# Splitting a turned block in two steps placed apart, and loading copied inputs ahead of copied states, in a recurrence and binary-FFN kernel

## The chip, the cores and the metric

The kernel runs on one core of one Trainium2 chip. The metric is the device time of one execution in microseconds (us). Three runs of the kernel before gave 456.02, 456.13 and 455.75 us; their median is 456.02 us.

## What is computed

`x` has shape (2, 4096, 256). A gated recurrence of state width 64 runs along the 4096 steps, its output is projected and normalised, and a feed-forward network with weights reduced to sign times mean magnitude follows.

```python
u = x @ W_in + b_in
g = sigmoid(x @ W_gate + b_gate)
h_t = tanh(h_prev @ A + u_t @ Bm)
y_t = h_t @ C.T + u_t @ D.T
y_t = g_t * y_t + (1.0 - g_t) * x_t
x1 = layernorm(x + (y @ W_out + b_out + x))
bw = mean(abs(w), axis=1) * sign(w)          # for w1 and for w2
h = gelu(x1 @ bw1.T + b1)                    # exact gelu, width 1024
out = layernorm(x1 + (h @ bw2.T + b2))
```

## The kernel before, in words

**Tiling.** The 4096 steps are cut into 64 segments of 64 steps that run side by side, so one recurrence step handles 2 x 64 columns at once. The plan is 48 warm-up steps and then 64 real ones. The 8192 rows of the output are worked on in 16 chunks of 512 rows (`NC` = 16, `SPC` = 4 recurrence steps to a chunk).

**Recurrence.** `steps` (L156) is one matmul of `ab` with the tile `st` (L157), which holds the states h in its upper 64 partitions and the inputs u in its lower 64, and one tanh on ACT that writes the next h (L158). The matmul of a step needs the tanh of the step before it.

**A chunk's stations.** `load` (L343) copies four steps of h and u out of `st` into `hu` by two DMAs. `mix` (L369) multiplies `hu` with `cd` into the PSUM tile `ps_y` (L374) and subtracts x into `d` on DVE (L381). `mix_end` makes y in the tile `tg` (L386, L389). `project` (L392) multiplies y with `w_out` into `ps_z` (L399), adds it into `xn` on DVE (L410) and takes the statistics of the first layernorm (`all_stats` L283: bn_stats L256, aggregate L260, variance plus eps L265, and a power of -1/2 on POOL L266). `shift` is a small DVE operation `nm_a` (L271), and `norm` applies scale and shift on ACT (L279). The normed block must then be turned. For chunks 2 to 14 `blocks` (L441) does this by a transpose within 32 x 32 blocks on DVE (`xb`, L446) and 16 DMAs of 32 KB from the SP queue (L452) that put the blocks in place in `xlo`. For the other chunks `turn` (L422) uses TensorE. `split` (L458) makes the high part `xhi`, a rounded copy on ACT (L460), and the low part, `xlo` minus `xhi`, on DVE (L461), in place.

**Feed-forward.** `up(g)` for g = 0 to 3 (L470) makes two tiles of hidden units: for each, products of the sign weights with `xhi` and then with `xlo` into `ps_h` (L479) and a gelu on ACT (L489), and after the second a rounded copy `hhi` on ACT (L500). `low(g)` (L503) makes `hlo` on DVE (L507). `down(g)` (L565) multiplies `hhi` and `hlo` into `ps_o` (L523), and after the last group `scale` writes `o` on DVE (L539). `add` (L543) adds it to the row, `stats` takes the second layernorm's statistics (`bs_b`, `rs_b`, `nm_b`), and `store` (L554) applies them on ACT (L279) and issues the output DMA (L560) on the SP queue. `rest` (L465) is an addition of a bias row on POOL.

**The order.** Every engine has one queue that it works off in order. Under `manual_schedule` (L689) the order on each is the order in which this Python code emits instructions. The loop over `c` (L759 to L818) works in iteration c on the FFN of chunk c, finishes the FFN of chunk c-1, mixes and projects chunk c+2, and normalises, turns and splits chunk c+1, which is "far" when 0 < c < 14 (L760). Four recurrence steps are emitted in an iteration by `step()` (L768, L779, L807, L812), named A, B, C and D here, until the plan is used up. In iteration c the matmul order is: up 0, step A, down 2 of c-1, mix of c+2, up 1, step B, down 3 of c-1, one gate tile (c from 1 to 12), up 2, step C, down 0, project of c+2, up 3, step D, down 1. `split` for chunk c+1 is called from within up 3, between its two gelus, through the argument `between` (L496, L811).

**Buffers named below.** `ps_h` rotates through 3 buffers that it shares with the gate tiles, `ps_y` and `ps_z` of the loop share one, `ps_o` has one, `h` has two, `xhi` and `xlo` two each, `hu` three.

**Before the loop**, gate tiles of later chunks are emitted in small pieces by `parts(n, pace)` between recurrence steps, and chunks 0, 1 and 2 are loaded by `next_steps` as soon as their states are there (L649 to L651).

## Time and profile before

| what | value |
|---|---|
| median of three runs | 456.02 us (455.75 to 456.13) |
| the profiled execution's own time | 453.23 us |
| its span, from first to last instruction | 451.5 us |
| TensorE matmul busy | 430.5 us, 95% of the span |
| VectorE (DVE) busy | 332.3 us, 74% |
| ScalarE (ACT) busy | 284.2 us, 63% |
| GpSimd (POOL) busy | 158.9 us, 35% |
| mean granted TensorE clock | 0.995 |
| share of DMA queue q1 in 16 engines' span | 35.4% |

The profiled execution lies 2.79 us below the median of the runs, so differences are worked out against 453.23 us and then carried over to the median. 1.73 us of the profiled time lie outside its span. A line of the profile's group view names the source line, the engine, the operation, the tile written and the tiles read, then busy time and the mean length of one in ns, then the idle time of the engine just before it and what ended that. PE is TensorE's matmul, PEld its weight load, SPq the SyncE queue that issues DMAs. In timelines the first number is the start in us from the span's start and the second the length. Matmul ends are modelled, so PE counts as busy also where it is not at its peak.

From one iteration to the next the kernel before takes 23.13 us (DVE's L461 starts at 127.75 us in iteration 1 and at 266.52 us in iteration 7).

### The profile page before, as it was taken

How to read it: one execution, taken by the hardware profiler on the slowest of the kernel's cores; microseconds unless marked ns; L12 is line 12 of the kernel's file. 1: busy time of each engine (PE TensorE's matmuls, PEld its weight loads, DVE VectorE, ACT ScalarE, POOL GpSimd, SP SyncE). 2: the span in 40 equal slices, each digit the busy share in tenths (PEclk: the TensorE clock that was granted, in tenths of full speed). 3: DMA queues.
4: the chain of work that ended last, by engine and by line, in shares of the span. 5: the costliest groups of instructions: out<-in, count | busy, mean ns of one | idle time of the engine just before them, and what ended most of it. 6: DMA issues, size and time to landing. Idle time of an engine off the chain costs nothing.

```text
span 451.5 us, 6834 instructions
## 1 busy us (share of the span) xinstructions
PE 430.5 (95%) x2402; PEld 344.3 (76%) x2402; DVE 332.3 (74%) x571; ACT 284.2 (63%) x476; POOL 158.9 (35%) x177
## 2 busy tenths in 40 slices
PE   9999998999999999999999999999999999988992
PEld 5665766788878787888878787878787878777982
DVE  0245937966979797878787888888787878785874
ACT  2443541577585859595858676767676767757681
POOL 1000500644352526161615261525252525241613
PEclk9999999999999999999999999999999999999998
DMA  8887514500253424252426241615142323210102
GB/s 300 301 276 256 216 23 131 173 1 6 54 161 70 185 65 143 59 195 53 158 46 213 45 166 42 215 42 169 40 131 77 95 69 87 74 64 1 46 1 99
DMA packets 31480, 51.34 MB, mean 114 GB/s; under 512 B 5329, under 2 KB 19665, under 8 KB 31441
## 3 DMA queue, kind: packets, MB, share of 16 engines
q1 hardware_dynamic: 30864, 50.48, 35.4%
q8 instruction: 21, 0.34, 0.4%
q10 hardware_dynamic: 576, 0.37, 0.3%
q14 instruction: 19, 0.15, 0.1%
HBM read 31.43 MB, written 8.39 MB: 88 GB/s over the span
## 4 chain that ended last, share of the span: by engine, by line
PE 40%; DVE 38%; issue 6%; POOL 5%; ACT 3%; SPq 3%; DMA 2%; DVEq 0%; POOLq 0%; ACTq 0%
PE ps_o L523 8%; PE ps_h L479 8%; PE ps_g L313 7%; PE ps_y L374 6%; POOL rs_b L266 5%; DVE bs_b L256 4%; PE ps_s L157 4%; DVE xlo L461 4%; DVE d L386 4%; PE ps_u L131 3%; DVE bs_a L256 3%; DVE o L539 3%; DVE d L381 3%; DVE xn L545 3%; DVE tg L389 3%
## 5 line engine op out<-in xcount | busy, mean ns | idle before, releaser
L489 ACT ACTIVATE h<-ps_h,bias_c,al 128x512 f32<-128x512 f32 x128 | 97.4, 776 | 39.6 <-PE ps_h L479 34.2
L523 PE MATMUL ps_o<-sg,hhi 128*128 128x256 f32 x496 | 121.5, 286 | 0.5 <-DVE o L539 0.5
L523 PE MATMUL ps_o<-sg,hlo 128*128 128x256 f32 x496 | 118.1, 279 | 0.1
L523 PEld LDWEIGHTS ps_o<-sg,hhi 128*128 128x128 f32 x496 | 93.5, 189 | 1.7 <-DVE o L539 0.9
L523 PEld LDWEIGHTS ps_o<-sg,hlo 128*128 128x128 f32 x496 | 93.5, 188 | 1.2 <-DVE hlo L507 0.4
L479 PE MATMUL ps_h<-xhi,sg 128*128 128x512 f32 x256 | 93.0, 445 | 0.5 <-ACT xhi L460 0.5
L479 PE MATMUL ps_h<-xlo,sg 128*128 128x512 f32 x256 | 81.5, 399 | 8.4 <-DVE xlo L461 8.2
L507 DVE TENSOR_TENSOR hlo<-h,hhi 128x1024 fp32r<-128x1024 f32 (+1 forms) x65 | 79.0, 1219 | 5.4 <-ACT hhi L500 5.3
L359 POOL TENSOR_TENSOR xn<-xn,bo_r 128x256 f32<-128x256 f32 x64 | 47.5, 774 | 84.8 <-DMA xn<-in_x 75.6
L266 POOL TENSOR_TENSOR rs_b<-rs_b,neg_half 128x4 f32<-128x4 f32 (+1 forms) x17 | 27.3, 1606 | 134.6 <-DVE rs_b L265 134.3
L500 ACT CAST hhi<-h 128x1024 fp32r<-128x1024 f32 (+1 forms) x65 | 67.5, 1040 | 2.0
L313 PE MATMUL ps_g<-xt,w_gate 128*128 128x384 f32 (+3 forms) x208 | 66.4, 431 | 0.0
L479 PEld LDWEIGHTS ps_h<-xlo,sg 128*128 128x128 f32 x256 | 47.1, 188 | 24.4 <-DVE xlo L461 13.8
L359 POOL TENSOR_TENSOR xn<-xn,b_r 128x256 f32<-128x256 f32 x64 | 61.6, 993 | 2.0 <-PE ps_t L427 2.0
L479 PEld LDWEIGHTS ps_h<-xhi,sg 128*128 128x128 f32 x256 | 46.5, 189 | 19.1 <-issue 11.2
L158 ACT ACTIVATE st<-ps_s 64x128 f32<-64x128 f32 x112 | 30.1, 268 | 47.6 <-PE ps_s L157 47.3
L399 PE MATMUL ps_z<-w_out,tg 128*128 128x256 f32 x256 | 58.2, 379 | 0.0
L157 PEld LDWEIGHTS ps_s<-st,wab 128*128 128x128 f32 x224 | 38.5, 189 | 22.4 <-ACT st L158 9.7
L279 ACT ACTIVATE xn<-xn,nm_b,rs_b 128x256 f32<-128x256 f32 x58 | 30.3, 594 | 40.1 <-DVE nm_b L271 40.1
L399 PEld LDWEIGHTS ps_z<-w_out,tg 128*128 128x128 f32 x256 | 47.2, 190 | 5.7
L157 PE MATMUL ps_s<-st,wab 128*128 128x128 f32 x224 | 43.9, 278 | 0.1
L381 DVE TENSOR_TENSOR d<-ps_y,xt 128x1024 f32<-128x1024 f32 x16 | 19.6, 1225 | 28.2 <-PE ps_y L374 28.2
(76 smaller groups left out, 465.3 us busy)
## 6 DMA issues: line engine op xcount, KB each, us to landing
xt<-in_xT SPq DMA_DIRECT2D x35, 512.0 KB, 4.3
xn<-in_x SPq DMA_DIRECT2D x16, 512.0 KB, 3.3
out_y<-xn SPq DMA_DIRECT2D x15, 512.0 KB, 2.6
xlo<-xb SPq DMA_DIRECT2D x208, 32.0 KB, 1.9
hu<-st SPq DMA_DIRECT2D x32, 128.0 KB, 2.3
w1t<-in_w1T SPq DMA_DIRECT2D x2, 512.0 KB, 5.8
w1n<-in_w SPq DMA_DIRECT2D x2, 512.0 KB, 7.4
w2t<-in_w2T SPq DMA_DIRECT2D x2, 512.0 KB, 6.0
```

The source lines that it names most:

```text
L157: nc.tensor.matmul(p_h, ab, st[:, j].rearrange("p b k -> p (b k)"), start=True, stop=True)
L256: nc.vector.bn_stats(self.bs[:, i, :], self.r[:, i, :])
L266: nc.gpsimd.tensor_tensor(rs, rs, neg_half[:, cut], ALU.pow)
L313: nc.tensor.matmul(ps[:, cut], w_gate[:, k, bass.ts(m, P)], xt_[:, k, cut], start=k == 0 and i == 0, stop=k == KD - 1, skip_group_check=True,)
L359: nc.gpsimd.tensor_tensor(r[:, i, :], r[:, i, :], row, ALU.add)
L381: nc.vector.tensor_sub(self.d, ps, xt_)
L399: nc.tensor.matmul(self.ps_z[:, i, :], self.y[:, k, bass.ts(i, P)], w_out[:, k, :], start=k == 0, stop=k == KD - 1,)
L479: nc.tensor.matmul(ps, sg1[:, k, bass.ts(j, P)], part[:, k, :], start=n == 0, stop=n == 2 * KD - 1,)
L489: nc.scalar.activation(to, ps.rearrange("p (a i c) -> p a i c", a=P // 32, c=32) if self.far else ps, AF.Gelu, bias=b1_c[:, j : j + 1], sc ...
L500: nc.scalar.copy(hi[:, part, :], h[:, part, :])
L507: nc.vector.tensor_sub(lo[:, i, :], h[:, i, :], hi[:, i, :].bitcast(FP))
L523: nc.tensor.matmul(ps[:, i, :], part[:, j % 2, bass.ts(tb, P)], sg2[:, j, :], start=j == 0 and part is self.h[j // 2][0] and first, stop=j ...
```

## The change

- `split` becomes `split_hi` (the ACT copy) and `split_lo` (the DVE subtraction). `split_hi` is emitted right after up 2, so on ACT it stands behind the copy `hhi` of up 2 and ahead of the store of chunk c-1; before, it stood between the two gelus of up 3.
- The statistics of the first layernorm leave `project` and become `stats1`. `split_lo` is emitted between the two, so on DVE the order is `xn` (L410), `xlo`, `bs_a`, where it was `xn`, `bs_a`, `mv_a`, `rs_a`, `xlo`.
- `low` of group 2 goes ahead of the store's shift `nm_b` on DVE.
- `load` becomes `load_u` and `load_h`. The u half is issued first; for chunks 0 to 2 it is issued with the `load_n` calls ahead of the last warm-up steps, and only the h half waits for the states.
- Ahead of the loop one piece of gate work moves: two pieces instead of one after the mix of chunk 0, and one instead of two after the projection of chunk 1.
- In iteration 13 `low` of group 0 goes ahead of the mix of chunk 15, and the four small DVE operations of `compare` move from iteration 13 to iteration 14.

The diff, cut to its core:

```diff
-        def load(self):
-            c, nm = self.c, self.nm
-            self.hu = xp.tile([P, N], FP, tag="hu", name=f"hu{nm}", bufs=3)
-            for r, src in (
-                (TOP, h_of[:, bass.ds(c * SPC + 1, SPC)]),
-                (LOW, u_of[:, bass.ds(c * SPC, SPC)]),
-            ):
-                nc.sync.dma_start(out=self.hu[r, :], in_=src.rearrange("p j b k -> p (j b k)"))
+        def load_u(self):
+            self.hu = xp.tile([P, N], FP, tag="hu", name=f"hu{self.nm}", bufs=3)
+            src = u_of[:, bass.ds(self.c * SPC, SPC)]
+            nc.sync.dma_start(out=self.hu[LOW, :], in_=src.rearrange("p j b k -> p (j b k)"))
+
+        def load_h(self):
+            src = h_of[:, bass.ds(self.c * SPC + 1, SPC)]
+            nc.sync.dma_start(out=self.hu[TOP, :], in_=src.rearrange("p j b k -> p (j b k)"))
 
         def load_n(self):
             c, nm = self.c, self.nm
...
             if half == 1:
                 x1 = self.x1 = self.xn
                 nc.vector.scalar_tensor_tensor(x1, self.xn, 2.0, self.ps_z, ALU.mult, ALU.add)
-                self.st1 = all_stats(x1, f"a{nm}")
+            yield
+
+        def stats1(self):
+            self.st1 = all_stats(self.x1, f"a{self.nm}")
             yield
 
         def shift(self):
...
                     )
             yield
 
-        def split(self):
+        def split_hi(self):
             self.hi = wk.tile([P, KD, N], FR, tag="xhi", name=f"xhi{self.nm}")
             nc.scalar.copy(self.hi, self.lo.bitcast(FP))
+            yield
+
+        def split_lo(self):
             nc.vector.tensor_sub(self.lo, self.lo.bitcast(FP), self.hi.bitcast(FP))
             self.h = {}
             self.far = True
+            yield
 
         def rest(self):
 
             self.add_row(self.x1, b2_r)
             yield
 
-        def up(self, g, apart=False, between=None):
+        def up(self, g, apart=False):
             nm = f"{self.nm}_{g}"
             h = wk.tile([P, 2, N], FP, tag="h", name=f"h{nm}")
             hi = wk.tile([P, 2, N], FR, tag="hhi", name=f"hhi{nm}", bufs=3)
...
                     bias=b1_c[:, j : j + 1],
                     scale=al1[:, j : j + 1],
                 )
-                if i == 0 and between is not None:
-                    between()
                 if i == 1:
                     for part in range(2) if apart else [slice(0, 2)]:
                         nc.scalar.copy(hi[:, part, :], h[:, part, :])
...
             first_states()
         for i in range(3):
             if done == WARM + (i + 1) * SPC:
-                ch[i].load()
+                ch[i].load_h()
         for what, args in waiting or ():
             what(*args)
         if waiting:
...
             need = WARM + (ch[i].c + 1) * SPC
             while done < need:
                 next_steps()
-            ch[i].load()
+            ch[i].load_u()
+            ch[i].load_h()
         elif what in ("load_n", "load_x", "load_gate_x"):
             getattr(ch[i], what)()
         else:
...
                 load_xT(n + 3)
                 for i in ((0,), (1, 2))[n - 5]:
                     ch[i].load_n()
+                    ch[i].load_u()
             for i in range(7 - before):
                 if 1 <= n < 5 and i == 0:
                     load_w(n - 1)
...
             ch[i].xt = x_tiles[i]
         do(0, "mix", pace=850)
         do(0, "mix_end")
-        parts(1, 600)
+        parts(2, 600)
         assert done >= WARM + 2 * SPC, done
         do(1, "mix", pace=850)
         do(1, "mix_end")
         parts(1, 600)
         do(0, "project", 0, p_2, "o", pace=1700)
         do(0, "project", 1, pace=1700)
+        do(0, "stats1")
         assert done >= WARM + 3 * SPC, done
         do(2, "mix", pace=1700)
         do(0, "shift")
         do(1, "project", 0, p_2, "o", pace=1700)
         do(0, "norm")
         do(1, "project", 1, pace=1700)
+        do(1, "stats1")
         mixed = ch[2].mix_end()
         next(mixed)
-        parts(2, 1700)
+        parts(1, 1700)
         while waiting:
             next_steps()
         waiting = None
...
             do(c, "up", 0)
             step()
             do(c - 1, "down", 2)
+            if c == end - 2:
+                do(c, "low", 0)
             if c > 0:
                 do(c + 2, "mix")
                 do(c + 2, "mix_end")
-            do(c, "low", 0)
+            if c != end - 2:
+                do(c, "low", 0)
+            if c == end - 1:
+                next(parts_met)
+                next(parts_met)
             do(c + 3, "load")
             do(c + 6, "load_x")
             if c % 2 == 0:
...
             if not far:
                 do(c + 1, "turn")
             do(c, "low", 1)
+            if c == end - 1:
+                next(parts_met)
+                next(parts_met)
             if not 1 <= c <= 12:
                 add()
             do(c + 1, "rest")
             do(c, "up", 2)
+            if far:
+                do(c + 1, "split_hi")
+            do(c, "low", 2)
             if c < end - 1:
                 do(c - 1, "store", range(TB), nc.scalar)
                 do(c + 3, "load_n")
-            do(c, "low", 2)
             if c == end - 1:
                 do(c - 1, "stats")
             if c == end - 2:
                 assert done == len(plan), done
-                next(parts_met)
-                next(parts_met)
             step()
             do(c, "down", 0)
             do(c + 2, "project", 0)
             do(c + 2, "project", 1)
-            do(c, "up", 3, False, ch[c + 1].split if far else None)
+            if far:
+                do(c + 1, "split_lo")
+            do(c + 2, "stats1")
+            do(c, "up", 3)
             step()
             do(c, "down", 1)
             if c == end - 1:
                 do(c - 1, "store")
-            if c == end - 2:
-                next(parts_met)
-                next(parts_met)
         count()
         do(end, "up", 0)
         do(end - 1, "low", 3)
```

More of the change, by code (lines that the diff above doesn't have):

```diff
@@ L619, in redo @@
             self.load_x()
-            self.load()
+            self.load_u()
+            self.load_h()
             self.load_n()
             pieces = [self.gate, self.mix, self.mix_end, lambda: self.project(0), lambda: self.project(1)]
+            pieces += [self.stats1]
             pieces += [self.shift, self.norm, self.turn, self.rest]
```

## Prediction

> **What bounds the kernel now.** I read the list of waits first, then the chain that ended last, then the timelines of ACT and SP. The waits show one thing that TensorE lacks in all thirteen far iterations (columns: us in total, times, longest):
>
> ```profile
> PE ps_h L479 <- DVE xlo L461: 8.2, 13, 2.7
> ACT xn L279 <- DVE nm_b L271: 40.1, 14, 4.6
> ```
>
> Up 0 has multiplied `xhi` and stands until `xlo` is made. ACT stands idle ahead of the store, which costs nothing by itself and is where the change puts the copy. The chain through iteration 7 (start, length) says why `xlo` is late:
>
> ```profile
> 244.67 1.65 PE ps_h L479 x6
> ...
> 248.44 1.73 PE ps_y L374 x4
> 250.19 1.24 DVE d L381
> ...
> 259.53 1.87 POOL rs_b L266
> ...
> 263.24 1.14 DVE xn L410
> 264.41 1.41 DVE bs_a L256 x4
> ...
> 266.52 1.24 DVE xlo L461
> ```
>
> A ring: `xlo` lets up 0 go on, `ps_y` feeds DVE, and DVE comes back to `xlo` 23.13 us later, with the statistics `bs_a` just ahead of it. Now ACT and SP in the same iteration:
>
> ```profile
> 258.46 1.06 ACT L500 CAST hhi<-h 128x1024 fp32r<-128x1024 f32 x1
> 262.14 2.09 ACT L279 ACTIVATE xn<-xn,nm_b,rs_b 128x256 f32<-128x256 f32 x4 [2.63 <-DVE nm_b L271]
> 264.13 0.26 ACT L158 ACTIVATE st<-ps_s 64x128 f32<-64x128 f32 x1
> ...
> 264.95 1.05 ACT L460 CAST xhi<-xlo 128x1024 fp32r<-128x1024 f32 x1
> ```
>
> ```profile
> 248.16 11.09 SPq L452 DMA_DIRECT2D xlo<-xb  x16
> ```
>
> The copy needs the last of 16 transfers, whose issue on SP takes 11.09 us. Here they had landed long before 264.95. The gap from 259.52 to 262.14 would hold the copy only if they land by about 261. Behind the store stands the tanh of step C (264.13), which step D on PE needs.
>
> **What the Trainium skill says.** "Perfetto Trace Analysis", under the DMA instruction by HWDGE: the profile shows a DMA's issue, and the movement of the data lies outside it. The page bears this out: the SP row is 0.59 us each, the landing 1.9 us. [...] "Perfetto Trace Analysis", Identifying Dependency Chains: an instruction that waits for several engines can have EventSemaphore instructions in front; `xlo` has four (52 for 13) and 0.23 us before it, which I keep.
>
> **The change, part by part.** U is the time at which up 0 would start with no wait inside it. Up 0 unhindered takes 1.83 us to the next step (up 3 of chunk 0, 105.55 to 107.38). In iteration 7 step A's product stands at 246.17, so U = 244.34. The matmul of up 0 really started at 243.72: the wait costs 0.62, and PE alone needs 23.13 - 0.62 = 22.51.
>
> (1) *Low part ahead of the statistics.* In iteration 7 `ps_z` starts 15.16 after U and is done 3.66 later (98.20 to 101.86), so `xn` starts at U + 18.82. `xlo` now comes 1.44 later (1.21 and the 0.23), at U + 20.26, and ends at U + 21.5; it was needed at U + 0.46 of the next iteration, which is U + 22.97. The wait is gone: 0.62 in nine iterations, 0.98 in one, 1.17 in two, 3.0 at the last; by the list 8.2 + 13 x 0.28 (the second half of a stall that the list doesn't count) = 11.8 us at most.
>
> (2) *What it delays.* The statistics stand behind `xlo`. From `bs_a` to the end of `xb` the trace has the same row of waits in iteration 1: 103.11 to 110.24 = 7.13 us (statistics, power on POOL, `nm_a`, four norms on ACT, transpose). So `xb` ends at 18.82 + 1.44 + 1.26 + 7.13 = 28.65 after U. I take 28.66, that is `xn` + 9.84. In iteration 7 it ended 3.76 after U (248.10); now 28.66 - 22.51 = 6.15 after the next U.
>
> (3) *The copy's new wait.* From `xb`'s end: 0.06 to SP, 10.49 to the last issue, 1.9 to land, 0.14 until the waiting engine starts (as 66.38 to 66.51), 0.95 copy, 1.99 store, 0.27 tanh C, 0.05 to PE: 15.85. Queued behind the waiting copy on ACT are the store, tanh C and both gelus of up 3; step D waits for tanh C, and down 1 and the next up 0 for step D. PE wants step D at U + 20.46 (264.80 in iteration 7, less the 0.62). 6.15 + 15.85 = U + 22.0: 1.5 late. But a late step D moves the next U and not `xn` of its own iteration, so that the following transpose comes early against its U. The closed path spans two iterations: U to `xn` 18.82, to `xb` 9.84, to step D 15.85, to the next U 2.05 + 0.19 for a restarted PE (93.05 to 93.38 against the usual 0.14). The sum is 46.75 per two, 23.375 an iteration against 23.13. The other resources hold. DVE's own ring through the norm, with `xlo` ahead of the statistics, sums from the same rows to 21.8. POOL ends its row additions (3.88 from U + 17.1) before the power at U + 23.6. The store moves with the copy and so does its output DMA on SP, by about 1.4; `load_n` behind it goes out some 4 us after it, still 3 us ahead of the next 16.
>
> (4) *Sum over the loop.* Iteration 1: `xb` ends at 110.24 as before and SP needs 12.0 there, so step D comes at 127.0 instead of 126.01: U(2) = 129.24 against 128.69, +0.55. Iterations 2 to 10: 210.25 against 208.56, +1.69. Iterations 11 and 12 have no steps (the last tanh in ACT's timeline is at 337.45), so the copy blocks no step; PE needs 22.86 - 1.17 = 21.69 each: 43.4 against 45.74, -2.36. Iteration 13: hlo of group 0 now waits for its hhi ahead of `d`. With `xb` at 389.6 the norm starts at 386.2, hhi ends at 390.7, `d` starts at 391.9 instead of 388.57, `o` frees `ps_o` at 396.8 instead of 394.6; then 1.94 down, 3.27 project, 3.9 up and down give the next U at 405.95 instead of 407.52: -1.5 on this step. Iteration 14: gelu 0 stands behind a norm that starts at 408.9 (before 408.35), and up 1's second tile waits for its buffer until 411.7: +1.1. Sum: 0.55 + 1.69 - 2.36 - 1.5 + 1.1 = -0.5.
>
> (5) *The u half.* The mixes of chunks 0 and 1 wait for the second of two DMAs:
>
> ```profile
> 68.74 2.25 DMA hu<-st
> 70.99 0.14 issue
> 71.13 1.10 PE ps_y L374 x2
> ```
>
> With u there, only the h half counts, issued 0.6 us sooner. Mix 0 loses its 0.27 of waiting, tanh 8 comes at 67.60, h lands at 70.2, mix 1 starts at 70.34 instead of 71.13, and the moved gate piece (0.87 with its step) fills the hole. -0.8, carried on by `ps_z`, `xn` and the rest of the chain. On SP the u loads stand ahead of `xt9` and `xn1`, needed some 20 us later: nothing, and the wait for u would have to last as long to cost any. The same order of halves in the loop: nothing, `hu` lands 8 us before its mix (262.8 against 271.3); without that cover 0.6 an iteration. The gate piece is PE work that is only moved.
>
> (6) *hlo 2 ahead of `nm_b`*: its hhi ends at U + 15.2 and `nm_b` waits for POOL to U + 17.05 anyway; nothing, and if that wait were gone 0.6 on the store, which waits for the copy. *compare* in iteration 14: 2.0 us of DVE into a gap of 3.45; nothing, at worst 2.0 if the gap closes.
>
> Sum: -0.5 - 0.8 = -1.3. 453.23 - 1.3 = 451.9 for an execution like the profiled one; with the 2.79 between it and the median, 454.8.
>
> **The unknown.** When 16 transfers have landed for a waiting ACT is not in the trace: nothing waited for the last one. From landings of 1.8 to 2.9 us (iteration 8), and 1.79 us for one issue in iteration 1, the path could be 0.1 shorter or 1.0 longer. Each 0.1 of it is 0.05 an iteration, and with iterations 11 to 13 about 0.65 in the sum. A gain beyond the 0.1 needs steps that I placed one after another to overlap, and isn't excluded.
>
> **The rivals.**
> *Copies in time (0.17).* The path over two iterations is 1.73 shorter than I sum it, or nearly; PE sets the pace at 22.51. For it: the gap of 2.63 ahead of the store. Against: it is the old `xb`'s. Then -0.63 - 9 x 0.62 - 0.37 - 2.36 - 0.4 (end) - 0.8 = -10.1: 445.9, and 446 to 453 in between.
> *Copies later (0.20), the slower side.* One mechanism: the last landing, seen from the head of ACT's queue, holds the store, tanh C and step D. It decides from 0.2 us beyond my path (-1.3 + 6.5 x 0.2 = 0); at 0.6 it is -1.3 + 3.9 = +2.6: 458.6. For it: the landings of 2.9. Against: the other DMAs of the loop are few at that time.
> *The gain of the end is lost (0.13).* If `d` in iteration 13 is later than 391.9 by the 1.3 that are over, all that is won goes there: 456.0.
> *The forecast (0.50)*: 453.0 to 456.5 by itself.
>
> **How the numbers follow.** 0.2% is 0.9 us, about what a measurement can tell from no change. Faster by more: most of the forecast case (0.38), copies in time (0.17) and a little of the end case (0.03) = 0.58. Within: 0.10 of the forecast, 0.08 of the end case, 0.02 of the slower = 0.20. Slower: 0.18 of the second rival and 0.02 each of the forecast and the end case = 0.22. The range leaves 0.1 on each side: 450.0, inside the first rival, and 458.5, at the second rival's price.
>
> **What would show it.** Right: no wait of L479 for `xlo`; ACT's copy waits for the `xlo` DMAs in iterations 1 to 10; step D waits for its tanh by 0.5 to 1 us; starts of up 0 23.3 to 23.5 apart to iteration 10 and 21.7 in 11 and 12; `xb` 5 us or more after U. Wrong: starts 22.5 apart (copies in time), or over 23.6 (copies later), or a chain through the first mixes that still shows the second hu DMA.

## The result, and the profile after

The changed kernel takes 450.39 us (median of 4 runs, 449.05 to 451.14); the kernel before, on the same chip, 456.07 us (455.75 to 458.65). The ratio is 0.986, 95% interval 0.982 to 0.990: 5.7 us less. The forecast was 1.3 us less, with a range of 450.0 to 458.5. The direction is right and the time lies at the lower edge of the range, but the gain is more than four times what I worked out.

The profiled execution after took 451.14 us, its span is 449.4 us. That is only 2.1 us below the profiled one before, while the medians are 5.7 apart. Both differences have to be explained.

The list of waits after (engine, line waited for, us in total, times, longest):

```profile
ACT xhi L463 <- DMA xlo<-xb: 30.3, 12, 4.8
PEld ps_s L157 <- ACT st L158: 16.0, 36, 1.3
ACT xn L279 <- DVE nm_b L271: 5.8, 4, 3.5
```

The line in which up 0 waited for the loop's `xlo` (8.2 us, 13 times) is gone. The copy now waits for the 16 transfers, as forecast. ACT's idle time ahead of the store fell from 40.1 to 5.8 us, because ACT now idles ahead of the copy instead (30.3 us). ACT and SP in iteration 7:

```profile
259.96 1.05 ACT L505 CAST hhi<-h 128x1024 fp32r<-128x1024 f32 x1
262.80 1.04 ACT L463 CAST xhi<-xlo 128x1024 fp32r<-128x1024 f32 x1 [1.79 <-DMA xlo<-xb]
264.28 2.08 ACT L279 ACTIVATE xn<-xn,nm_b,rs_b 128x256 f32<-128x256 f32 x4 [0.43 <-DVE nm_b L271]
```

```profile
250.37 11.12 SPq L455 DMA_DIRECT2D xlo<-xb  x16
```

The copy stands at the head of ACT's queue until 262.80, behind it the store and the tanh of step C (266.26 here). DVE in the same iteration:

```profile
241.39 1.22 DVE L410 SCALAR_TENSOR_TENSOR xn<-xn,ps_z 128x1024 f32<-128x1024 f32 x1 [0.89 <-PE ps_z L399]
242.53 1.22 DVE L467 TENSOR_TENSOR xlo<-xlo,xhi 128x1024 fp32r<-128x1024 f32 x1
243.66 1.40 DVE L256 BATCH_NORM_STATS2 bs_a<-xn 128x6 f32<-128x256 f32 x4
...
246.74 0.16 DVE L271 SCALAR_TENSOR_TENSOR nm_a<-mv_a,rs_a 128x4 f32<-128x4 f32 x1 [1.20 <-POOL rs_a L266]
...
249.06 1.25 DVE L449 STREAM_TRANSPOSE xb<-xn 128x1024 f32<-128x1024 f32 x1 [1.02 <-ACT xn L279]
```

`xlo` follows `xn` at once, and from the start of `xn` to the end of `xb` it is 241.39 to 250.31 = 8.92 us. Over iterations 2 to 10 it is 8.9 in eight and 9.3 in one. The prediction had 9.84.

The start of the row `ps_z` (L399, 16 products) marks each iteration on TensorE, so the difference can be laid out by stretches (us; "after" and "again" are differences from before, "again" is a second profile of the changed kernel, span 446.6, from the runs below; the ten iterations run from the `ps_z` of iteration 0 to that of iteration 10):

| stretch | before | forecast | after | again |
|---|---|---|---|---|
| start to the first `ps_z` of the loop | 98.20 | -0.8 | +1.97 | +0.64 |
| ten iterations from there | 231.07 | +2.24 | -1.25 | -2.21 |
| the two without steps | 45.40 | -2.36 | -1.80 | -1.81 |
| the rest | 76.78 | -0.4 | -1.02 | -1.42 |
| span | 451.5 | -1.3 | -2.1 | -4.8 |

Part of the row "start" is there before any edit has an effect: the steps at 20 to 64 us lie a constant 0.37 us later than before in the first profile and 0.06 earlier in the second. The forecast counted from up 0 to up 0, not from `ps_z` to `ps_z`. That moves waits from one stretch to the next, so its terms are set against what they measured, counted its way, in the part on the prediction.

### The profile page after: what moved, and what is told of

It is laid out like the page before. It is cut to its first block, busy times and chain, and to the rows that moved or that the text cites. A ratio compares the mean times of both kernels' runs of the same rounds, so it can differ in the third digit from the quotient of the medians.

```text
span 449.4 us, 6825 instructions
## 1 busy us (share of the span) xinstructions
PE 428.2 (95%) x2402; PEld 344.2 (77%) x2402; DVE 332.0 (74%) x571; ACT 284.4 (63%) x476; POOL 152.5 (34%) x177
## 4 chain that ended last, share of the span: by engine, by line
PE 61%; DVE 12%; SPq 9%; ACT 8%; DMA 4%; issue 3%; POOL 2%; POOLq 0%; DVEq 0%; ACTq 0%
PE ps_o L528 15%; PE ps_h L486 14%; PE ps_g L313 10%; SPq L455 9%; PE ps_z L399 8%; PE ps_s L157 5%; PE ps_y L374 5%; ACT xn L279 4%; PE ps_u L131 3%; DVE hlo L512 2%; DMA xt<-in_xT 2%; DMA hu<-st 1%; ACT h L496 1%; DMA xlo<-xb 1%; DVE bs_a L256 1%
## 5 line engine op out<-in xcount | busy, mean ns | idle before, releaser
L496 ACT ACTIVATE h<-ps_h,bias_c,al 128x512 f32<-128x512 f32 x128 | 95.7, 772 | 27.8 <-PE ps_h L486 23.5
L486 PE MATMUL ps_h<-xlo,sg 128*128 128x512 f32 x256 | 80.1, 393 | 1.3 <-DVE xlo L440 1.2
L359 POOL TENSOR_TENSOR xn<-xn,bo_r 128x256 f32<-128x256 f32 x64 | 50.5, 820 | 82.8 <-DMA xn<-in_x 77.5
L399 PE MATMUL ps_z<-w_out,tg 128*128 128x256 f32 x256 | 58.2, 379 | 0.0
L486 PEld LDWEIGHTS ps_h<-xlo,sg 128*128 128x128 f32 x256 | 48.1, 188 | 12.8 <-DVE xlo L440 2.1
L359 POOL TENSOR_TENSOR xn<-xn,b_r 128x256 f32<-128x256 f32 x64 | 51.3, 831 | 2.0 <-PE ps_t L430 2.0
L399 PEld LDWEIGHTS ps_z<-w_out,tg 128*128 128x128 f32 x256 | 47.2, 190 | 5.7
L266 POOL TENSOR_TENSOR rs_a<-rs_a,neg_half 128x4 f32<-128x4 f32 x16 | 17.2, 1076 | 72.5 <-DVE rs_a L265 69.3
L279 ACT ACTIVATE xn<-xn,nm_a,rs_a 128x256 f32<-128x256 f32 x60 | 31.2, 591 | 14.6 <-DVE nm_a L271 14.6
```

Source lines behind the costliest of these rows:

```text
L266: nc.gpsimd.tensor_tensor(rs, rs, neg_half[:, cut], ALU.pow)
L279: nc.scalar.activation(r, r, AF.Identity, bias=self.sh[:, i : i + 1], scale=rs)
L359: nc.gpsimd.tensor_tensor(r[:, i, :], r[:, i, :], row, ALU.add)
L399: nc.tensor.matmul(self.ps_z[:, i, :], self.y[:, k, bass.ts(i, P)], w_out[:, k, :], start=k == 0, stop=k == KD - 1,)
L486: nc.tensor.matmul(ps, sg1[:, k, bass.ts(j, P)], part[:, k, :], start=n == 0, stop=n == 2 * KD - 1,)
L496: nc.scalar.activation(to, ps.rearrange("p (a i c) -> p a i c", a=P // 32, c=32) if self.far else ps, AF.Gelu, bias=b1_c[:, j : j + 1], sc ...
```

## The experiments

All runs of one group were on one chip, beside the kernel before. Its median was 454.68 us beside the first four experiments below, 455.38 beside the next four (from "The changed kernel again"), 454.84 beside the next four kernels (from "The copy alone") and 454.87 beside the last two.

### The kernel before again

No edit.

> The kernel before, unchanged, against itself. Both theories expect a ratio of 1.000. The question is how far a profiled execution stands from the timed ones: the profiled execution of before was 453.23, its timed ones 455.75 to 456.13. If the 2.8 between them is a property of that one execution, the time and the span of this run lie near 456 and its profile shows where the 2.8 went; if profiled executions are always quicker, this one is near 453 again. The first case would say that the pair of profiles (2.1 apart) understates the gain, the second that the medians (5.7 apart) overstate it.

454.55 us, ratio 0.999 (0.997 to 1.001), as it should be. The span of its profile is 453.3 us against 451.5, and up to the last `ps_z` it is even 0.5 us ahead (396.05 against 396.58). From there it takes 57.3 us instead of 54.9. The place shows when that stretch is cut into windows. Columns: window, its us, then busy time and instructions of PE, PEld, DVE, ACT and POOL, the granted clock of TensorE, the DMA share, GB/s. First the profile that the prediction used, then this one:

```profile
404.00:407.00 3.00, 0.73 (x2) 0.30 (x2) 2.70 (x11) 2.12 (x3) 0.50 (x1) 1.00 0.31 123
407.00:409.00 2.00, 1.14 (x5) 0.96 (x6) 1.97 (x5) 0.65 (x2) 0.52 (x1) 1.00 0.00 0
409.00:411.00 2.00, 2.00 (x17) 1.92 (x16) 0.45 (x1) 2.00 (x4) 0.00 (x0) 1.00 0.00 0
```

```profile
404.00:407.00 3.00, 0.64 (x2) 0.20 (x2) 2.73 (x10) 1.57 (x2) 1.02 (x1) 0.80 0.13 52
407.00:409.00 2.00, 1.69 (x4) 1.40 (x5) 1.87 (x5) 1.19 (x3) 0.00 (x0) 0.50 0.00 0
409.00:411.00 2.00, 2.00 (x8) 1.71 (x8) 0.00 (x0) 2.00 (x4) 0.00 (x0) 0.50 0.00 0
```

In both, TensorE stands nearly idle while up 0 of chunk 14 waits for `xlo` (0.7 us of work in 3 us). In the second, the granted clock falls to 0.50 within that wait, and TensorE then gets through 8 instructions in 2 us instead of 17. The profile that I predicted from had escaped this. So a wait that the change removes costs more in other executions than in the one I read. The runs without a profile say the same: of 124 executions of the kernel before on the four chips, 9 show the mean clock of 0.995 that the first profile has, and they took 452.4 to 453.5 us; the other 115 show less and took 453.9 to 458.7.

### The u half alone

```diff
-                ch[i].load()
+                ch[i].load_h()
...
                     ch[i].load_n()
+                    ch[i].load_u()
...
-        parts(1, 600)
+        parts(2, 600)
...
-        parts(2, 1700)
+        parts(1, 1700)
```

> Only the u half of the copied states first, with the gate piece that goes with it; the copy, the low part, the statistics and the end are as before. My theory: mix 1 starts 0.8 sooner and all that follows with it, so 455.3 against 456.1. Rival: the landing of the h half decides and is not sooner, so that nothing changes (456.1), or the added queue makes it worse by up to 1 as in the profile of the changed kernel, where one landing took 3.51. A third theory gives it most of the 5.7: then 452 or less.

455.37 us, ratio 1.000 (0.998 to 1.002): nothing. In its profile mix 1 no longer waits, and the first `ps_z` row starts at 73.42 against 74.24; but TensorE was 0.38 ahead at 57 us already, before the edit touches anything, so 0.44 of the forecast 0.8 was won. Then it is lost again: the first `ps_z` of the loop starts at 98.56 against 98.20. How shows in the second profile of the changed kernel, below.

### The loop's part alone

```diff
             do(c, "up", 2)
+            if far:
+                do(c + 1, "split_hi")
+            do(c, "low", 2)
...
-            do(c, "low", 2)
...
-            do(c, "up", 3, False, ch[c + 1].split if far else None)
+            if far:
+                do(c + 1, "split_lo")
+            do(c + 2, "stats1")
+            do(c, "up", 3)
```

> Only the loop's part of the change (copy behind up 2, low part ahead of the statistics); the loads of u and the order at the end are as before. My prediction's sum for the loop was -0.5, so about 455.6. My theory now, with the path over two iterations shorter by the 1.0 to 1.1 that the profile of the changed kernel shows between xn and xb and at the landing: iterations 1 to 10 win about 1.2 instead of losing 2.2, iterations 11 and 12 win 1.8, iteration 13 and the end about 1, so -3.5 to -4.5: 452. Rival: the loop gives little (455.5) and the u half and the end give the rest.

447.52 us, ratio 0.983 (0.980 to 0.986). The whole gain, and more, is in the loop's part. By stretches against before: ten iterations -2.12, the two without steps -1.81, the rest -1.51, start -0.32, together 5.8 us of span against the profile of before that kept its clock, 7.6 against the one that did not; the medians differ by 7.2.

### The copy behind the tanh of step C

```diff
             do(c, "up", 2)
-            if far:
-                do(c + 1, "split_hi")
             do(c, "low", 2)
             ...
             step()
+            if far:
+                do(c + 1, "split_hi")
```

> The changed kernel, with the copy of the turned block moved on ACT from ahead of the store and of the tanh of step C to just behind that tanh. My theory: the wait for the last of the 16 transfers no longer holds step C's tanh and step D, so TensorE sets the pace and iterations 2 to 10 take 22.5 to 22.6 instead of 23.04: 4 to 5 us less than the changed kernel, about 445.5. Rival: the copy is then made so late that the low part is late for up 0 again and the statistics behind it with it, so that the same 23.0 or more stand there: 450 to 452.

457.48 us, ratio 1.0055 (1.004 to 1.007): slower than before, a miss for both theories. Ten iterations take 232.36. ACT and DVE in one of them:

```profile
265.04 2.08 ACT L279 ACTIVATE xn<-xn,nm_b,rs_b 128x256 f32<-128x256 f32 x4 [3.96 <-DVE nm_b L271]
267.02 0.25 ACT L158 ACTIVATE st<-ps_s 64x128 f32<-64x128 f32 x1
267.18 1.03 ACT L463 CAST xhi<-xlo 128x1024 fp32r<-128x1024 f32 x1
```

```profile
264.92 1.21 DVE L410 SCALAR_TENSOR_TENSOR xn<-xn,ps_z 128x1024 f32<-128x1024 f32 x1
268.24 1.23 DVE L467 TENSOR_TENSOR xlo<-xlo,xhi 128x1024 fp32r<-128x1024 f32 x1 [2.11 <-ACT xhi L463]
```

The copy now stands behind the store, the store waits for `nm_b`, and `xlo` waits for the copy with the statistics, `xb` and all of DVE's later work, `nm_b` among it, behind it: a ring of DVE and ACT from `xlo` at 244.17 to `xlo` at 268.24, 24.07 us, one of the longest turns. Over iterations 2 to 10 it is 23.32 in the mean. The edit moved the copy past two instructions where only one was in dispute, so it says nothing on the dispute.

### The changed kernel again

No edit.

> The changed kernel once more, beside the next three on one chip. Its ratio to before was 0.986 (0.982 to 0.990); its loop's part alone gave 0.983. My theory: 0.987 again, 449 to 451, with the start 1 to 2 later than in the loop's part alone. If its first profile only had an unlucky landing of 3.51 at the start, this one shows the 2.3 of an ordinary landing there and starts iteration 1 some 1.2 sooner.

448.64 us, ratio 0.986 (0.983 to 0.989), the same as on the first chip. Its span is 6.7 us below that of the kernel before in `b_again` (a profile from another chip), just as its median is below that of before. ACT at the start:

```profile
77.62 0.69 ACT L365 ACTIVATE tg<-ps_g,bg_c 128x512 f32<-128x512 f32 x1 [3.41 <-PE ps_z L399]
78.20 0.26 ACT L158 ACTIVATE st<-ps_s 64x128 f32<-64x128 f32 x1
```

```profile
78.52 0.49 PE L157 MATMUL ps_s<-st,wab 128*128 128x128 f32 x2 [0.93 <-ACT st L158]
```

A tanh of the gates stands 3.41 us on ACT until the projection of chunk 0 has ended, a step's tanh stands behind it, and TensorE waits 0.93 us for that.

### The order of the end undone

```diff
-            if c == end - 2:
-                do(c, "low", 0)
             ...
-            if c != end - 2:
-                do(c, "low", 0)
+            do(c, "low", 0)
```

with the two `next(parts_met)` pairs at their old places.

> The changed kernel with the order of the end as before: low part of group 0 of iteration 13 behind the mix again, and the comparison of states where it was. My prediction had these at nothing or better. In the profiles iteration 13 takes 22.38 in the changed kernel and 21.74 without the new order, and the stretch behind it is the same (53.4 and 53.5). Theory: the moved low part costs 0.6, so 0.6 less than the changed kernel. Rival: no difference that can be measured.

448.68 us, ratio 0.985 (0.982 to 0.988): no difference that can be measured. Iteration 13 takes 21.70 instead of 22.10 us, and TensorE waits 1.48 instead of 1.82 us for `o` there, so the moved low part seems to cost some 0.4 in it. The start of its profile was 1.4 us later, as its second h half took 3.74 us to land where the changed kernel's second profile has 2.19.

### The gate piece back at its place

```diff
         do(0, "mix_end")
-        parts(2, 600)
+        parts(1, 600)
...
         next(mixed)
-        parts(1, 1700)
+        parts(2, 1700)
```

> The changed kernel, with the gate piece back behind the second half of the projection (u still loaded first). In the profile of the u part alone mix 1 and the projection start 0.8 sooner, as predicted, but then a tanh of the gates (the 3.41 of waiting for ps_z ahead of it) stands on ACT before a step's tanh and TensorE waits 0.93 for that. My theory: this tanh belongs to the moved gate piece and waits for the buffer that the projection of chunk 0 still reads; with the piece back, the hold of 0.93 is gone and the 0.8 stays, so 0.9 to 1.8 less than the changed kernel. Rival: mix 1 waits for its h half again as long as the piece filled, and the gain of 0.8 is lost with it: no difference.

447.55 us, ratio 0.983 (0.980 to 0.986), 1.1 us less than the changed kernel, though the intervals overlap. The profile is clearer: the wait of 0.93 us is gone, and the first `ps_z` of the loop starts at 97.59 instead of 98.84. The chain at the start shows two more things (start, length):

```profile
63.34 3.17 DMA hu<-st
...
68.30 2.18 DMA hu<-st
```

The first h half takes 3.17 us to land, where every profile with the old loads has 2.34 or 2.35. The second one is quick.

### The tanh of step C ahead of the copy

```diff
             do(c, "up", 2)
+            step()
             if far:
                 do(c + 1, "split_hi")
             do(c, "low", 2)
             ...
-            step()
             do(c, "down", 0)
```

> The changed kernel, with the tanh of step C put on ACT ahead of the copy and the store; nothing else moves, TensorE's order is the same. My theory: the 4 to 5 us that step D waits for this tanh in iterations 2 to 10 is the copy's new wait, and the path over two iterations as resized is 45.7, that is 22.9 an iteration; with the tanh of step C free the path goes through the tanh of step D, which has 1.8 more room, so 22.0, and TensorE decides with 22.51: 4 less than the changed kernel, 446. Rival: it is another wait (the copy itself on DVE, as where it was put behind the tanh), and the pace stays at 23.0: no difference.

445.37 us, ratio 0.978 (0.975 to 0.981), 3.3 us less than the changed kernel. Iterations 1 to 10 take 22.50 or 22.51 us each, with no exception. ACT now:

```profile
255.08 1.05 ACT L505 CAST hhi<-h 128x1024 fp32r<-128x1024 f32 x1
256.04 0.26 ACT L158 ACTIVATE st<-ps_s 64x128 f32<-64x128 f32 x1
258.53 1.04 ACT L463 CAST xhi<-xlo 128x1024 fp32r<-128x1024 f32 x1 [2.23 <-DMA xlo<-xb]
259.88 2.08 ACT L279 ACTIVATE xn<-xn,nm_b,rs_b 128x256 f32<-128x256 f32 x4 [0.30 <-DVE nm_b L271]
```

The copy waits for its transfers as long as before (2.23), but nothing that TensorE needs soon stands behind it. Over iterations 2 to 10 the first profile of the changed kernel had this line among its waits, and here it is gone:

```profile
PEld ps_s L157 <- ACT st L158: 5.4, 7, 1.1
```

This settles the prediction's third step: the copy does hold step D, and the hold costs what TensorE's 22.51 and the measured pace differ by. Not all of it arrives at the end: iteration 13 takes 23.02 instead of 22.10, because TensorE, idle for 1.91 us until `o` comes, goes on at half the clock for 3.4 us.

### The copy alone

The statistics again ahead of the low part, against `loop_only`:

```diff
+            do(c + 2, "stats1")
             if far:
                 do(c + 1, "split_lo")
-            do(c + 2, "stats1")
```

> The kernel before, with the copy of the turned block behind up 2, but the statistics still ahead of the low part (u half, gate piece and end as before). My theory: without the low part's delay xb ends 3.76 after U, its last transfer is there at about U + 16.3, and the copy fits into the gap of 2.6 ahead of the store; the statistics then still hold xlo by the 0.62 an iteration of the kernel before, so nothing is won or lost: 454 to 455.5, ratio 0.998 to 1.000, with 23.0 to 23.13 an iteration. Rival: the early copy itself is worth something (ACT's up 3 is freed of it), and a good part of the loop's 7 comes from it: below 452.

452.78 us, ratio 0.995 (0.993 to 0.997). Ten iterations take 230.89, as before: in these the early copy (and `low` 2 ahead of `nm_b`, which this kernel has too) is worth nothing, and up 0 waits for `xlo` 8 times, 3.0 us in all, in iterations 2 to 10. The 2 us come later: 0.34 in the two iterations without steps, 0.34 in iteration 13 and 0.87 behind it in this profile. A part can be the clock, as 9 of its 22 runs have 0.995 or more, against 3 of 27 of the kernel before beside it.

### The step's tanh first, in the loop's part alone

The edit of `step_first`, on `loop_only`.

> The loop's part of the change alone (copy behind up 2, low part ahead of the statistics; u half, gate piece and end as before), with the tanh of step C ahead of the copy and the store on ACT. Theory: 22.51 in each of iterations 2 to 10 as in the same edit of the whole change, so 4 less than the loop's part alone (ratio 0.983), ratio 0.974, 443.5. Rival: with the other order at the end iteration 13 takes up what is won, and the ratio stays near 0.978.

443.35 us, ratio 0.9755 (0.971 to 0.980). Again 22.51 in each iteration, and iteration 13 takes 21.17 with the old order.

### Three edits together, with the new and the old order of the end

Against the changed kernel: `step_first`, the gate piece back, and

```diff
                 for i in ((0,), (1, 2))[n - 5]:
                     ch[i].load_n()
+                for i in ((0,), (1, 2))[n - 5]:
                     ch[i].load_u()
```

> The changed kernel with three edits: tanh of step C ahead of the copy on ACT, gate piece back behind the projection, and the first three loads of u behind the loads of xn of the same stage. Theory for the third: the load of u of chunk 1 waits on SP until that u is made (60.8), and holds the 512 KB load of xn behind it, so that this load runs when the first h half is to land: mix 0 then waits 0.47 instead of 0.27 and starts 3.3 after the issue of the h half instead of 2.5 after the issue of the last half. With the xn loads ahead again h lands in 2.3, mix 0 and mix 1 start some 0.5 to 0.8 sooner than with u first so far, and iteration 1 starts at 96.8 to 97.2 on the span's clock. With 22.51 an iteration the time is about 444 and the ratio 0.975. Rival: the landing is no sooner, and the start stays at 97.6: ratio 0.9765.

> As the last, with the order of the end as in the kernel before (low part of group 0 of iteration 13 behind the mix, the comparison of states where it was). Theory: with the new order iteration 13 took 22.1 to 23.0, with the old one 21.7, and what follows takes the same: 0.4 to 1.3 less, about 443. Rival: the last stretch gives it back, and there is no difference.

444.38 us (ratio 0.9755, 0.972 to 0.980) and 442.86 us (0.9725, 0.969 to 0.976). Both beat the changed kernel; the second is the fastest of all, though its interval overlaps those of its neighbours. The new order of the loads did what it was to do for the first mix, which no longer waits, and its h half landed in 2.19 and 2.18, but then the second h half landed in 3.67 and 3.63 us, and the start won nothing. With the new order of the end iteration 13 took 23.81 with a clock of 0.50, with the old one 21.26.

### Work for an idle TensorE

Ten products into a tile that nobody reads, in the kernel before:

```diff
                         stop=n == 2 * KD - 1,
                     )
+                    if isinstance(self.c, int) and self.c == NC - 2 and j == 0 and n == KD - 1:
+                        idle_products(10)
```

> The kernel before, with ten products of ones by ones (128 columns each, some 0.24 us apiece in the kernel's first row of the kind) put on TensorE inside up 0 of chunk 14, between the pair that multiplies xhi and the pair that waits for xlo; their result is read by nobody. They stand in the 2.69 us in which TensorE waits there for xlo, and take nothing from it. Theory: it is that idle stretch which lets the granted clock fall to 0.50 behind it in most executions of the kernel before (in two of the three profiles with this stretch, which then end 1.5 to 2.3 later), and so a part of the changed kernel's gain, which removes the wait. Then this kernel is faster though it only adds work: 452.5 to 453.5 against 454.7 to 455.4, ratio 0.995 to 0.997, and its profile shows the clock at 1.00 there. Rival: the clock falls for another reason (the time since the start, or the load), and the ratio is 1.000 or above.

453.06 us (452.71 to 455.46), ratio 0.997 (0.996 to 0.999): the kernel before becomes 1.2 us faster by the ratio, 1.8 by the medians, through ten products whose result nobody reads. Of its 8 runs 7 show a mean clock of 0.993 or more, of the 29 of the kernel before beside it 1. The last stretch takes 54.9 us, as in the undisturbed profile, with

```profile
404.00:407.00 3.00, 2.85 (x22) 2.68 (x22) 2.70 (x11) 1.82 (x3) 0.81 (x1) 1.00 0.22 87
407.00:409.00 2.00, 1.55 (x8) 1.22 (x7) 1.97 (x5) 0.95 (x2) 0.21 (x1) 1.00 0.00 0
```

### The u half alone, the gate piece left where it was

The loads of `u_only`, without its `parts`.

> The kernel before, with u loaded first and nothing else: the gate piece stays where it was. With the piece moved the ratio was 1.0003 (0.998 to 1.002). Theory: mix 1 starts 0.3 to 0.8 sooner and no tanh of the gates is in the way, so 0.3 to 0.8 less than before, ratio 0.9985. Rival: the h half lands in 3.2 to 3.7 instead of 2.2, as it did in several starts with u first, and takes it all: 1.000.

453.89 us, ratio 0.999 (0.9975 to 1.001): not to be told from nothing. In its profile the first h half lands in 3.19 us and the second in 2.19, and the first `ps_z` of the loop starts at 97.23. But this profile was 0.55 ahead of the first one of before already at 57 us, so the start won some 0.4.

## Why the prediction was too small

**Low part ahead of the statistics (step 1): right.** The wait of up 0 is gone from all thirteen iterations. `copy_only` shows that this, not the early copy, is what the ten iterations gain by.

**What it delays (step 2): the mechanism right, the size wrong, and this is the step that failed.** "I take 28.66, that is `xn` + 9.84"; the profile has 8.92. Two terms were wrong. From `xn` to `bs_a` I had 1.44 + 1.26 = 2.70 and it took 2.27. Of this, 0.23 is the idle time ahead of `xlo` that I kept. The four instructions in front of `xlo` are still there in twelve of thirteen iterations, but they now follow `xn`, which takes 1.22 us, and not `rs_a`, which takes 0.17, and no idle time is left. From `bs_a` to the end of `xb` I took 7.13 from iteration 1, and it took 6.65. `nm_a` alone was 0.70 us there and is 0.16 here. Iterations 1 and 7 of the kernel before:

```profile
106.07 3.89 POOL L359 TENSOR_TENSOR xn<-xn,bo_r 128x256 f32<-128x256 f32 x4
106.13 0.70 DVE L271 SCALAR_TENSOR_TENSOR nm_a<-mv_a,rs_a 128x4 f32<-128x4 f32 x1 [1.13 <-POOL rs_a L266]
244.54 0.16 DVE L271 SCALAR_TENSOR_TENSOR nm_a<-mv_a,rs_a 128x4 f32<-128x4 f32 x1
```

In the profiles of before, after and `step_first` each of the 90 instructions of L271 takes 0.68 to 0.70 when one of POOL's row additions (L359) runs at that moment and 0.14 to 0.17 when none does. In iteration 1 POOL starts one 0.06 us earlier; in iterations 2 to 13, before as after, it has nothing to do then. So the row that I took was the only one of thirteen with the long `nm_a`, and the same row in iteration 7 was 6.8 already. The Trainium skill agrees on the kind of cause, "Trainium Architecture — The Big Picture", What this means for kernel authors: VectorE and GpSimd share one pair of ports, held by one at a time. That it is the port here, no run shows.

**The copy's new wait (step 3): right.** A step D that waits closes a path over two iterations, and the trace gives its parts. Means over eight pairs of iterations of the second profile, with the forecast in brackets: from step D to the next `xn` 20.95 (21.06), from there to the end of `xb` 8.91 (9.84), from there to step D 15.98 (15.85), together 45.84 (46.75), that is 22.92 an iteration (23.375). So the whole difference is the term of step 2. The last landing to the copy took 0.02 to 0.31, 0.18 in the mean (I took 0.14). The 22.92 is a mean: single iterations take 22.5, TensorE's own pace, to 23.4. I had named 0.1 less as one end of the unknown and of a gain beyond it only said that it "isn't excluded". `step_first` shows that the path is this one: with the tanh of step C off it, the pace is TensorE's 22.51.

**The sum over the loop (step 4).** Its terms, counted its way (here between the starts of the last product of up 0), against what they measured:

| term | forecast | after | again |
|---|---|---|---|
| up to iteration 1 | -0.8 | +1.97 | +0.64 |
| iteration 1 | +0.55 | +0.29 | +0.26 |
| iterations 2 to 10 | +1.69 | -2.15 | -3.10 |
| iterations 11 and 12 | -2.36 | -2.35 | -2.35 |
| iteration 13 | -1.5 | -2.1 | -2.45 |
| from there to the end | +1.1 | +2.3 | +2.2 |

The large miss is iterations 2 to 10, 3.8 and 4.8 us. Step 2 makes nearly half a us of it in each, and iteration 10, which I had at the path's pace, took 22.5, TensorE's own. (9 x 23.375 is 210.4 and not my 210.25, a slip of 0.1.) Iterations 11 and 12 came as forecast. Iteration 13 and the end had the right signs, and both were too small. In iteration 13 TensorE waits for `o`, 2.15 and 1.82 us in the two profiles. That the measured time lies in the range is no merit of the sum: the loop gave more than forecast, the start took a part of it back, and the clock, below, was not in it.

**The u half (step 5): failed.** -0.8 was forecast and nothing was won: ratio 1.000 alone. Mix 1 did start sooner, by 0.44. "The gate piece is PE work that is only moved" left out its tanh: it writes a gate tile that the projection of chunk 0 still reads, so it waits 3.41 us on ACT and holds a step, 0.93 on TensorE. "On SP the u loads stand ahead of `xt9` and `xn1`" left out that SP waits there until the u of chunk 1 exists; the 512 KB load behind it then goes out at 61.37 and is under way together with the first h half, which takes 0.8 longer to land. In `best`, where that load goes out before, the h half takes 2.19. Putting the piece back gave 1.1 us, with intervals that overlap.

With the old loads the second h half lands in 2.18 to 2.21 us. With u first it needs 2.18 or 2.19 in five profiles and 3.2 to 3.7 in five, the first one of the changed kernel among them. The traces show what the late landings have in common: in each of the five a packet of 16 KB of DMA queue q8, which the profile lists as "instruction", starts 1.0 us after the h half was issued, and in the other five none is under way. It is the same with the 32 KB transfers of `xlo`. Of the 3328 in the sixteen profiles, 2558 have no packet of an instruction queue (q8 or q14) under way, and all of these land in 1.83 to 2.04 us. All 473 that take more than 2.1, up to 4.0, have one. No run moved these packets, so the link is one of time; but no late landing is without one.

**The steps at no cost (step 6).** The comparison moved and `hlo` moved: no cost to be seen, apart from the 0.4 in iteration 13.

**What was not in the sum at all.** 453.23 us was an execution that had kept its clock. "With the 2.79 between it and the median" I carried a difference over as if both kernels had it. Part of it was a cost of the wait that the change removes: of the four profiles that have that idle stretch as it was (`before`, `b_again`, `u_only`, `u_only_nopiece`), three take 1.5 to 2.4 us longer behind the last `ps_z`, and filling the stretch gained 1.2 in the mean. So the second profile of the changed kernel is 4.8 below an execution that kept its clock and 6.7 below one that did not.

The account in one line, from the second profile: -1.3 forecast, +1.4 for the start, -0.3 for iteration 1, -4.8 for iterations 2 to 10, -0.95 for iteration 13 and +1.1 for the end make -4.8; the 1.9 between the spans of the two profiles of before, which is 2.4 by the clock less the 0.5 by which the second was ahead, makes -6.7, which is also the difference of the medians on that chip.

Of the rivals, none came as described; the time fell in the gap between "copies in time" and the forecast, for the reason of the first: the path was shorter than I summed it.

## What to carry to other kernels

When an instruction is moved to where it waits for a transfer, list what is queued behind it on its engine and let the urgent, short ones go first: one line moved (the step's tanh ahead of the copy) was worth 3.3 us here. A duration borrowed from another iteration holds only if the other engines do the same beside it; compare at least two rows before summing, since here one other row would have shown that the long `nm_a` was an exception. One profile is also only one execution: the one read here had kept its clock, and 115 of 124 others had not. And a moved piece of work takes its activations and its buffers along: ask who still reads the buffer that it writes.

## What the hardware did that I had not expected

An idle stretch of TensorE can cost twice: 2.7 us of waiting in the kernel before, then half the clock for 3.4 us (`u_only`, `u_only_nopiece`) or 6.8 us (`b_again`) in three of four profiles. The same followed idle stretches of 1.91 and 2.06 us in iteration 13 of `step_first` and `best`, but neither one of 2.15 in the first profile of the changed kernel nor one of 2.62 in `copy_only`.

The traces show what decides. In all sixteen the first stretch at full clock lasts a whole multiple of 3.413 us, for example 112 times that in `step_first` and 118 times in `u_only`. It begins 3.9 to 6.9 us after the start of the span, at another time in each execution. Cut on this grid, the sixteen profiles have 2045 windows that begin at full clock. The share of a window in which PE is busy tells how it ends:

| window | busy share | clock behind it |
|---|---|---|
| `u_only`, 404.25 to 407.66 | 0.21 | 0.50 |
| `best`, 384.37 to 387.78 | 0.40 | 0.50 |
| `step_first`, 384.98 to 388.39 | 0.44 | 0.50 |
| `after_again`, 389.67 to 393.08 | 0.49 | 1.00 |
| `b_again`, 402.41 to 405.82 | 0.50 | 0.50 |
| before, 402.85 to 406.26 and the next | 0.53, 0.53 | 1.00 |
| `copy_only`, 401.51 to 404.92 and the next | 0.58, 0.65 | 1.00 |
| after, 389.57 to 392.98 and the next | 0.68, 0.69 | 1.00 |

All windows below 0.45 ended in a fall and none above 0.51 did (22 falls in all, 16 of them at the end of a kernel, where TensorE has no more work). Of the four between, three kept the clock and one lost it; the ends of the products are modelled, so the limit can't be told more closely. What counts, then, is how much of the wait lies in one window. In the profile of before the wait lay across two, with 0.53 in each, and that was luck. The Trainium skill, "TensorE: Matmul & The Clock Gate", Part 1: The HAM clock gate, says that half rate comes after an idle window of about 3.4 us, and that the windows run free of the kernel, so that it depends on where one falls. The length of the window and the chance in it agree with the traces; that a window has to be idle does not, since here one that was 0.44 busy was enough. Ten products whose result nobody reads were a gain.
